# A four-layer graph network on one core: x by chunks of nodes, f1 through DRAM, and the last 20 keys in three copies

## Chip, core and metric

The kernel runs on one NeuronCore of a Trainium2 chip, in float32. The metric is the device time of one execution in microseconds. A profile is of one further execution; its engines are PE (TensorE's products, PEld its weight loads), DVE (VectorE), ACT (ScalarE), POOL (GpSimd) and SP (SyncE, which here only issues DMAs).

## The reference, cut to what matters

There are 2708 nodes with 512 features, a 0/1 adjacency matrix and four layers, each ended by a residual and a layer norm. Only layer 0 is changed. It has four heads of 128 features:

```python
Xw = einsum('hnd,hde->hne', Xh, W)            # 4 heads, 128 x 128 each
f1 = einsum('hnd,hd->hn', Xw, V[:, 0, :, 0])  # one number per node and head
f2 = einsum('hnd,hd->hn', Xw, V[:, 1, :, 0])
sig = sigmoid(f1[:, :, None] + f2[:, None, :])
att = masked_softmax(adj * sig, adj != 0)     # both patterns are adj
Xa = einsum('hij,hjd->hid', att, Xw)          # first attention pass
emb = mlp_block(batchnorm(Xa))                # x @ W.T, elu, residual, batch norm
Y = einsum('hij,hjd->hid', att, emb)          # second attention pass, same att
# times W.T per head, elu, a second mlp_block; then x = layernorm(x + out)
```

Layers 1 to 3 (a plain graph convolution, an attention masked by adj, an attention with adj as a bias) follow and are left as they are, but for one helper tile.

## The kernel before

The 2708 nodes make 22 blocks of 128 keys, the last of them with 20 (`BLOCKS`). Scores are held transposed: keys on the partitions, queries in the free dimension. The queries are cut in two halves of 1354 (`HSPAN`), a half in three chunks of 452, 450 and 452 (`HCH`, and `CHUNKS` for all six).

**project** (L186 to L251) makes what the attention needs. SP loads the small weights, then x transposed, as four transfers of one feature block with all 2708 nodes each (L197). From `w0T` and the two vectors it forms the products W·v (L200), and copies W·v1 to 128 columns (`wv1`, L205). Six float32 products with those columns (L210; a float32 product leaves two records in the trace, so twelve) give f1 of the first two heads and the first half directly broadcast over all 128 partitions, in `f1b`. For all six chunks, products with 32 of the columns (L218) give f1 in rows, and POOL's queue writes them to DRAM (`f1_d`, L227). Then, block by block, L232 gives xw with f2 beside it: ACT copies two of three blocks to `xw`, DVE the third (L240), and DVE keeps f2 in `f2h` (L244). Three PSUM buffers take turns.

**attention_pass** (L270) is run twice, with `xw` and then with `emb` as values. For each half `hf` and each pair of heads `p` it goes over the 22 key blocks. `form` (L294) loads the block's 0/1 rows `a` from adj transposed; in the first pass at p = 0 ("prepare") DVE turns zeros into -1e30 (L303, L304) and POOL's queue writes the result to `adj_d`, from which later rounds load. ACT forms tanh of f1 + f2 for both heads (L313), DVE adds and multiplies by `a` (L321), ACT takes the exponential (L322). The result `t` (four buffers) has 128 keys by 2 heads by 1354 queries. L366 multiplies it: two heads by three chunks, each accumulating in its own bank of PSUM over all 22 blocks. In the first pass, products with ones (L389) sum the exponentials: after each block at p = 0, after pairs of blocks else. A few `t` are kept in DRAM in the first pass and loaded back in the second (`KEPT`, L358 and L360; the last block is among them for every round of the second pass). `f1b` of every round but the first comes from `f1_d` by a broadcasting DMA (L330).

At the end of a round `keep` (first pass) copies the six banks to `ft` on DVE and ACT (L466), and `decode` (second pass) scales them on DVE (L660) and runs the following products and elus. The next round's products take the same six banks.

The last block's products in before, for any block:

```python
values[:n, jt, h * P : (h + 1) * P],
t[:n, k, q0 : q0 + qw],
```

With n = 20 they use rows 0 to 19 of the array. Layers 2 and 3 already hold the last 20 rows of their values in several copies, at partitions 0, 32, 64 and 96 (`values4`, L947 to L950), and multiply each copy in its own row group (L1090). A helper tile `quarters` is made from `ident` at L878 to L885.

The order on each engine comes from a scheduler over the tile framework; instructions of an engine run in that order, and each waits for semaphores. SP's DMAs are issued in SP's order. Tiles of one tag take turns in `bufs` buffers; `enc_w` (L183) shares its buffer with `held`, so its load waits for the last product that reads `held`.

Of the kernel before, what the change touches and what calls it, by code (L numbers as in the profile page):

```python
# [8 lines left out]
F32 = mybir.dt.float32  # L9
# [8 lines left out]
P = 128  # L18
# [11 lines left out]
def gnn_stack_kernel(  # L30
# [33 lines left out]

    const = ctx.enter_context(tc.tile_pool(name="const", bufs=1))
# [6 lines left out]
    nc.sync.dma_start(prm_sb, prm)  # L72
# [78 lines left out]
    with ExitStack() as l0:  # L151
# [20 lines left out]
        f2h = p0.tile([P, NT, H], F32, name="f2h")  # L172

        bm1 = p0.tile([P, C], F32, name="bm1")
        nc.vector.tensor_scalar(bm1, prm_sb[:, MB_DEC, :], 1.0, None, ALU.subtract)
        w0T_sb = p0.tile([P, H, P], F32, name="w0T_sb")
        nc.sync.dma_start(w0T_sb, w0T)
# [8 lines left out]
        def project(att, psum):  # L186

            held = p0.tile([P, C, F], F32, tag="mlp_w", name="held").rearrange("p c f -> p (c f)")  # L190
            w0x = held[:, : H * (P + 2)].rearrange("p (h e) -> p h e", h=H)
            nc.sync.dma_start(w0x[:, :, :P], w0)
            v12 = att.tile([P, H, 2], F32, tag="v12", name="v12", bufs=1)
            nc.sync.dma_start(v12[:, :, 0], v1)
            nc.sync.dma_start(v12[:, :, 1], v2.rearrange("(h e) -> e h", h=H))
            for c in range(C):
                nc.sync.dma_start(xT_sb[:, c, :], xT[c * P : (c + 1) * P, :])  # L197
# [6 lines left out]
            wv1 = held[:, H * (P + 2) : H * (2 * P + 2)].rearrange("p (h e) -> p h e", h=H)  # L204
            nc.vector.tensor_copy(wv1, w0x[:, :, P : P + 1].to_broadcast([P, H, P]))  # L205
            f1b = att.tile([P, HP, HW], F32, tag="f1b", name="f1b")
            for k in range(HP):
                for q, (q0, w) in enumerate(HCH[0]):
                    pf = psum.tile([P, HP, BANK], F32, tag=f"po{q}", name="pf")[:, k, :]
                    nc.tensor.matmul(  # L210
                        pf[:, :w], wv1[:, k, :], xT_sb[:, k, q0 : q0 + w], start=True, stop=True
                    )
                    copy = nc.scalar.copy if q % 2 else nc.vector.tensor_copy
                    copy(f1b[:, k, q0 : q0 + w], pf[:, :w])
            for ci, (c0, w) in enumerate(CHUNKS):
                pf = psum.tile([P, BANK], F32, tag=f"psm{ci % 2}", name="pf")
                for h in range(H):
                    nc.tensor.matmul(  # L218
                        pf[32 * h : 32 * h + 32, :w],
                        wv1[:, h, :32],  # L220
                        xT_sb[:, h, c0 : c0 + w],
                        start=True,
                        stop=True,
                    )
                f1c = att.tile([P, BW], F32, tag="rs", name="f1c")
                nc.vector.tensor_copy(f1c[:, :w], pf[:, :w])
                nc.gpsimd.dma_start(f1_d[:, c0 : c0 + w], f1c[0 : 32 * H : 32, :w])  # L227
# [23 lines left out]
            return f1b  # L251
# [18 lines left out]
        def attention_pass(values, first, att, psum, finish, f1b=None):  # L270
# [23 lines left out]
            def form(hf, p, jt, att, prepare, f1b, tv):  # L294
# [3 lines left out]
                a = att.tile([P, HW], F32, tag="a", name="a", bufs=4 if first else 3)  # L298
                src = adjT if prepare else adj_d
                nc.sync.dma_start(a[:n, :w], src[j0 : j0 + n, h0 : h0 + w])  # L300
                if prepare:
# [5 lines left out]
                    nc.gpsimd.dma_start(adj_d[j0 : j0 + n, h0 : h0 + w], a[:n, :w])  # L307
# [17 lines left out]
            for hf, (h0, w) in enumerate(HSPAN):  # L325
                for p in range(H // HP):
                    prepare = first and p == 0
                    if f1b is None or not prepare or hf > 0:
                        f1b = att.tile([P, HP, HW], F32, tag="f1b", name="f1b", bufs=2)
                        nc.sync.dma_start(  # L330
                            f1b[:, :, :w],
                            f1_d[HP * p : HP * (p + 1), h0 : h0 + w].partition_broadcast(P),
                        )
# [13 lines left out]
                    for jt, (j0, n) in enumerate(BLOCKS):  # L347
# [7 lines left out]
                        if kept is None or first:  # L355
                            form(hf, p, jt, att, prepare, f1b, tv)
                            if kept is not None:
                                nc.gpsimd.dma_start(kept[:n, :, :w], tv)  # L358
                        else:
                            nc.sync.dma_start(tv, kept[:n, :, :w])  # L360
                            if p == 0 and jt in KEPT[1]:
                                count(hf, jt, att)
                        for k in range(HP):
                            h = HP * p + k
                            for q, (q0, qw) in enumerate(HCH[hf]):
# [1049 lines left out]
```

## Time and profile before

| what | us |
|---|---|
| three runs | 3385.58, 3387.1, 3390.83 |
| their median | 3387.1 |
| the profiled execution, its own time | 3383.28 |
| its span, first to last instruction | 3381.5 |
| PE busy in the span | 3304.0 |
| first product of L366 starts at | 53.72 |
| L366 in the first pass, 1056 records, busy | 433.0 |
| L366 in the second pass, 1056 records, busy | 416.3 |
| DVE L321, 162 instructions, busy | 479.3 |
| mean granted PE clock (share of full speed) | 0.984 |

Times within the profile are counted from the span's start. Busy times of groups are unions, so overlapping records aren't counted twice, while the mean of one record is its own length; a PE record's end is modelled. A wait is put down to the engine or transfer whose signal came last.

### The profile page before, as it was taken

How to read it: one execution, taken by the hardware profiler on the slowest of the kernel's cores; microseconds unless marked ns; L12 is line 12 of the kernel's file. 1: busy time of each engine (PE TensorE's matmuls, PEld its weight loads, DVE VectorE, ACT ScalarE, POOL GpSimd, SP SyncE). 2: the span in 40 equal slices, each digit the busy share in tenths (PEclk: the TensorE clock that was granted, in tenths of full speed). 3: DMA queues.
4: the chain of work that ended last, by engine and by line, in shares of the span. 5: the costliest groups of instructions: out<-in, count | busy, mean ns of one | idle time of the engine just before them, and what ended most of it. 6: DMA issues, size and time to landing. Idle time of an engine off the chain costs nothing.

```text
span 3381.5 us, 30504 instructions
## 1 busy us (share of the span) xinstructions
PE 3304.0 (98%) x10981; PEld 1761.1 (52%) x10981; DVE 1988.8 (59%) x3227; ACT 1339.6 (40%) x1491; POOL 127.6 (4%) x205
## 2 busy tenths in 40 slices
PE   8999999999999989999999999999999999999998
PEld 4444444544444445886555555444455555555554
DVE  7867977767687585445136666777253442543533
ACT  6877887568858743001133333333011010110110
POOL 1100100000000000000010000000000000000001
PEclk9998999999999999999999999999999999999999
DMA  7655753335524331550034444554111111111100
GB/s 279 246 164 166 276 184 114 120 103 168 184 82 160 126 106 61 140 136 19 0 114 125 116 127 128 145 148 112 58 50 35 44 33 44 37 33 44 35 23 19
DMA packets 167483, 364.03 MB, mean 108 GB/s; under 512 B 20374, under 2 KB 111194, under 8 KB 164100
## 3 DMA queue, kind: packets, MB, share of 16 engines
q1 hardware_dynamic: 152596, 298.43, 29.3%
q0 software_dynamic: 14736, 63.66, 5.0%
q8 instruction: 86, 1.41, 0.2%
q14 instruction: 65, 0.53, 0.0%
HBM read 298.34 MB, written 63.35 MB: 107 GB/s over the span
## 4 chain that ended last, share of the span: by engine, by line
PE 74%; issue 15%; DVE 6%; DMA 2%; ACT 2%; POOL 1%; SPq 0%; POOLq 0%; DVEq 0%; ACTq 0%
PE po L1090 22%; PE ps_s L996 17%; PE po L366 8%; PE ps_nb L842 7%; PE ps_wide L908 4%; PE ps_hid L113 2%; PE ps_sup L1233 2%; DVE t L321 2%; PE ps_o L1168 2%; PE ps_dec L687 2%; PE ps_mlp L601 1%; DMA a<-adj_d 1%; POOL adj_d L307 1%; PE ps_s L991 1%; ACT t L313 1%
## 5 line engine op out<-in xcount | busy, mean ns | idle before, releaser
L321 DVE SCALAR_TENSOR_TENSOR t<-t,a 128x2708 f32<-128x2708 f32 (+1 forms) x162 | 479.3, 2975 | 144.8 <-ACT t L313 143.3
L313 ACT ACTIVATE t<-f1b,f2h 128x1354 f32<-128x1354 f32 (+1 forms) x324 | 445.3, 1414 | 91.2 <-PE psm L389 47.1
L366 PE MATMUL po<-t,xw 128*128 128x452 f32 (+3 forms) x1056 | 433.0, 561 | 3.9 <-ACT t L322 3.9
L366 PE MATMUL po<-t,emb 128*128 128x452 f32 (+3 forms) x1056 | 416.3, 552 | 10.7 <-ACT t L322 9.2
L322 ACT ACTIVATE t<-t 128x2708 f32<-128x2708 f32 (+1 forms) x162 | 396.7, 2452 | 52.0 <-DVE t L321 50.5
L1090 PE MATMUL po<-sup,e 128*128 128x512 f32 x882 | 410.0, 601 | 5.2 <-DVE e L1277 5.2
L1090 PE MATMUL po<-e,xs 128*128 128x384 f32 (+1 forms) x1176 | 407.5, 489 | 0.0
L996 PE MATMUL ps_s<-q,hT 128*128 128x384 f32 (+1 forms) x1176 | 403.5, 489 | 0.0
L1331 DVE SCALAR_TENSOR_TENSOR e<-a_cols,ps_s 128x384 f32<-128x384 f32 (+1 forms) x154 | 85.6, 556 | 419.7 <-PE ps_s L996 396.6
L366 PEld LDWEIGHTS po<-t,emb 128*128 128x128 f32 (+1 forms) x1056 | 201.6, 193 | 220.1 <-issue 199.2
L366 PEld LDWEIGHTS po<-t,xw 128*128 128x128 f32 (+1 forms) x1056 | 197.8, 193 | 224.9 <-issue 211.4
L996 PEld LDWEIGHTS ps_s<-q,hT 128*128 128x128 f32 x1176 | 222.6, 190 | 161.5 <-issue 6.2
L1090 PEld LDWEIGHTS po<-e,xs 128*128 128x128 f32 x1176 | 221.6, 190 | 157.2 <-issue 6.0
L1090 PEld LDWEIGHTS po<-sup,e 128*128 128x128 f32 x882 | 162.0, 192 | 176.8 <-issue 148.3
L996 PE MATMUL ps_s<-hT 128*128 128x384 f32 (+1 forms) x672 | 229.2, 488 | 1.0 <-ACT sup L1240 0.7
L93 ACT ACTIVATE ln_rstd<-ln_rstd 128x1 f32<-128x1 f32 x88 | 17.2, 201 | 497.4 <-DVE ln_rstd L92 496.9
L1273 ACT ACTIVATE a_cols<-a_cols,neg_big 128x384 f32<-128x384 f32 (+1 forms) x154 | 94.8, 616 | 249.7 <-DMA a_cols<-in_adjT_dram 208.4
L842 PE MATMUL ps_nb<-hid_hi,at 128*128 128x512 f32 x484 | 188.1, 390 | 0.4 <-DVE at L836 0.4
L842 PE MATMUL ps_nb<-hid_lo,at 128*128 128x512 f32 x484 | 187.8, 389 | 0.0
L1067 ACT COPY nmax<-pb 128x384 f32<-128x384 f32 (+1 forms) x14 | 6.7, 479 | 430.5 <-PE pb L1054 349.8
L996 PEld LDWEIGHTS ps_s<-hT 128*128 128x128 f32 x672 | 125.8, 190 | 97.1 <-issue 18.0
L1085 DVE TENSOR_TENSOR acc<-acc,e 128x384 f32<-128x384 f32 (+2 forms) x294 | 162.9, 554 | 12.3 <-ACT e L1075 2.3
(223 smaller groups left out, 3474.1 us busy)
## 6 DMA issues: line engine op xcount, KB each, us to landing
a<-adj_d SPq DMA_DIRECT2D x116, 677.0 KB
a_cols<-in_adjT_dram SPq DMA_DIRECT2D x378, 192.0 KB
a<-in_adjT_dram SPq DMA_DIRECT2D x42, 677.0 KB
adj_d<-a POOLq DMA_DIRECT2D x42, 677.0 KB, 4.5
raw<-in_adjT_dram SPq DMA_DIRECT2D x105, 256.0 KB
kept<-t POOLq DMA_DIRECT2D x10, 1354.0 KB, 6.6
t<-kept SPq DMA_DIRECT2D x10, 1354.0 KB
a_cols<-in_adjT_dram SPq DMA_DIRECT2D x63, 202.0 KB
```

The lines of the kernel that those rows point to most:

```text
L113: nc.tensor.matmul(ps[:n], xt[:, c, :n], w[:, c, :], start=(c == 0), stop=(c == C - 1))
L313: nc.scalar.activation(tv[:, k, :], f1b[:n, k, :w], AF.Tanh, bias=f2h[:n, jt, h : h + 1], scale=0.5,)
L321: nc.vector.scalar_tensor_tensor(tv, tv, GUARD, ab, ALU.add, ALU.mult)
L322: nc.scalar.activation(tv, tv, AF.Exp, scale=0.5)
L366: nc.tensor.matmul(po[HB * k + q][:, :qw], values[:n, jt, h * P : (h + 1) * P], t[:n, k, q0 : q0 + qw], start=(jt == 0), stop=(jt == NT - 1),)
L842: nc.tensor.matmul(pos[it], at, half[:, jt, :], start=(jt == 0 and k == 0), stop=(jt == NT - 1 and k == 1),)
L908: nc.tensor.matmul(ps[:, :width], w(c, o), xt(c), start=(c == 0), stop=(c == C - 1),)
L996: nc.tensor.matmul(ps[:, :w], keys[:, c, j0 : j0 + P], st["q"][:, c, :], start=(c == 0), stop=(c == C - 1),)
L1085: nc.vector.tensor_tensor(acc, acc, e[:m], ALU.add)
L1090: nc.tensor.matmul(out, lhsT, rhs, start=(k == 0), stop=(k == NT - 1))
L1273: nc.scalar.activation(a, a, AF.Identity, bias=neg_big[: a.shape[0]], scale=1.0e30)
L1331: nc.vector.scalar_tensor_tensor(e, a, 2.0, ps, ALU.mult, ALU.add)
```

## The change

Three things are done in layer 0.

- **x and the vectors.** The two vectors are the first loads, then the weights, then x in six chunks of nodes with all features of each (one transfer a chunk), with the first two blocks of `a` put between them. `prm` comes after that.
- **f1.** The broadcast products of L210 are gone. f1 of the first three chunks is formed in rows first, then all blocks of xw, then f1 of the other three. The first three chunks go to DRAM by SP's queue, the others by POOL's, and `f1b` of every round, the first too, comes back by a broadcasting DMA.
- **The last 20 keys.** xw, f2h and emb of the last block get two more copies at partitions 32 and 64, made by DMAs on POOL's queue from one part of SBUF to another. The tile `a` of the last block is loaded in three copies, with rows of other keys to fill the 12 rows between them; tanh, the vector steps and the exponential then run on 84 rows. A kept `t` is loaded three times. Of the products of a head, chunk q uses copy q, in rows 32q to 32q + 19.

The tile `quarters` moves from the pool that lives throughout to one that opens after layer 1.

The diff, cut to its core (`Q` = 32, `REST` = 20, `HB` = 3, `HR` = 84):

```diff
+        nc.vector.memset(f2h[:, NT - 1, :], 0.0)
+        HR = (HB - 1) * Q + REST
+        def copies(rows):
+            for r in range(1, HB):
+                nc.gpsimd.dma_start(rows[r * Q : r * Q + REST], rows[:REST])
...
-            nc.sync.dma_start(w0x[:, :, :P], w0)
             v12 = att.tile([P, H, 2], F32, tag="v12", name="v12", bufs=1)
-            nc.sync.dma_start(v12[:, :, 0], v1)
             nc.sync.dma_start(v12[:, :, 1], v2.rearrange("(h e) -> e h", h=H))
-            for c in range(C):
-                nc.sync.dma_start(xT_sb[:, c, :], xT[c * P : (c + 1) * P, :])
+            nc.sync.dma_start(v12[:, :, 0], v1)
+            nc.sync.dma_start(w0T_sb, w0T)
+            nc.sync.dma_start(w0x[:, :, :P], w0)
+            blocks = []
+            for ci, (c0, w) in enumerate(CHUNKS):
+                nc.sync.dma_start(
+                    xT_sb[:, :, c0 : c0 + w],
+                    xT[:, c0 : c0 + w].rearrange("(c p) j -> p c j", p=P),
+                )
+                if HB - 1 <= ci and len(blocks) < 2:
+                    j0 = P * len(blocks)
+                    a = att.tile([P, HW], F32, tag="a", name="a", bufs=4)
+                    nc.sync.dma_start(a[:, : HSPAN[0][1]], adjT[j0 : j0 + P, : HSPAN[0][1]])
+                    blocks.append(a)
+            nc.sync.dma_start(prm_sb, prm)
+            nc.vector.tensor_scalar(bm1, prm_sb[:, MB_DEC, :], 1.0, None, ALU.subtract)
...
-            f1b = att.tile([P, HP, HW], F32, tag="f1b", name="f1b")
-            for k in range(HP):
-                for q, (q0, w) in enumerate(HCH[0]):
-                    pf = psum.tile([P, HP, BANK], F32, tag=f"po{q}", name="pf")[:, k, :]
-                    nc.tensor.matmul(
-                        pf[:, :w], wv1[:, k, :], xT_sb[:, k, q0 : q0 + w], start=True, stop=True
-                    )
-                    copy = nc.scalar.copy if q % 2 else nc.vector.tensor_copy
-                    copy(f1b[:, k, q0 : q0 + w], pf[:, :w])
-            for ci, (c0, w) in enumerate(CHUNKS):
+            def f1_rows(ci):
...
-                nc.gpsimd.dma_start(f1_d[:, c0 : c0 + w], f1c[0 : 32 * H : 32, :w])
+                queue = nc.sync if ci < HB else nc.gpsimd
+                queue.dma_start(f1_d[:, c0 : c0 + w], f1c[0 : 32 * H : 32, :w])
+            for ci in range(HB):
+                f1_rows(ci)
             for jt, (j0, n) in enumerate(BLOCKS):
...
-            return f1b
+            for ci in range(HB, NCH):
+                f1_rows(ci)
+            copies(xw[:, NT - 1, :])
+            copies(f2h[:, NT - 1, :])
+            return blocks
...
+                if n < P:
+                    for r in range(HB):
+                        if r > 0:
+                            nc.sync.dma_start(
+                                a[r * Q : r * Q + n, :w], src[j0 : j0 + n, h0 : h0 + w]
+                            )
+                        if r + 1 < HB:
+                            nc.sync.dma_start(
+                                a[r * Q + n : (r + 1) * Q, :w], src[: Q - n, h0 : h0 + w]
+                            )
+                    n = HR
...
-                    if f1b is None or not prepare or hf > 0:
-                        f1b = att.tile([P, HP, HW], F32, tag="f1b", name="f1b", bufs=2)
+                    f1b = att.tile([P, HP, HW], F32, tag="f1b", name="f1b", bufs=2)
...
-                            nc.sync.dma_start(tv, kept[:n, :, :w])
+                            for r in range(0, P if n == P else HB * Q, P if n == P else Q):
+                                nc.sync.dma_start(t[r : r + n, :, :w], kept[:n, :, :w])
...
+                                r = 0 if n == P else q * Q
                                 nc.tensor.matmul(
                                     po[HB * k + q][:, :qw],
-                                    values[:n, jt, h * P : (h + 1) * P],
-                                    t[:n, k, q0 : q0 + qw],
+                                    values[r : r + n, jt, h * P : (h + 1) * P],
+                                    t[r : r + n, k, q0 : q0 + qw],
...
+            copies(emb[:, NT - 1, :])
...
-    quarters = const.tile([P, C, Q], F32, name="quarters")
+    quarters = featp.tile([P, C, Q], F32, name="quarters")
```

## The prediction

> I call one run over the 22 key blocks for one half of the columns and one pair of heads a quarter: A1 to A4 are those of the first attention pass in the kernel's order, B1 to B4 those of the second. Line numbers are those of the kernel before.
>
> **What bounds the kernel now.** First the page's busy times:
>
> ```profile
> PE 3304.0 (98%) x10981; PEld 1761.1 (52%) x10981; DVE 1988.8 (59%) x3227; ACT 1339.6 (40%) x1491; POOL 127.6 (4%) x205
> ```
>
> TensorE nearly always has work, so time goes only where PE work goes, runs faster, or waits less. The change touches layer 0, up to about 1240 us. So second, the waits there: from 53 to 620 us PE waits 6.3 us in all, and ScalarE waits for PE:
>
> ```profile
> PE po L366 <- ACT t L322: 3.9, 6, 1.2
> ...
> ACT t L313 <- PE psm L389: 47.1, 42, 6.2
> ```
>
> (total, times, longest.) Pass A is PE's. From 680 to 1240 us PE waits 9.2 us for the exponentials (L322) and 7.9 us for the decoder's vector chain: in pass B, PE and ScalarE are close.
>
> Third, PE's timeline at the end of A1 (start, duration, ..., shape, records; a float32 product leaves two records), and the windows around it, where the third number from the right is the granted clock:
>
> ```profile
> 176.07 1.35 PE L389 MATMUL psm<-t,ones 128*32 128x340 f32 x16
> 177.35 5.89 PE L366 MATMUL po<-t,xw 20*128 20x452 f32 x12
> 183.17 2.49 PE L389 MATMUL psm<-t,ones 20*32 20x340 f32 x16
> ```
> ```profile
> 177.00:180.00 3.00, 3.00 (x15) 1.40 (x8) 0.21 (x1) 2.76 (x2) 0.00 (x0) 1.00 0.58 175
> 181.00:185.00 4.00, 4.00 (x20) 1.03 (x18) 2.41 (x5) 2.18 (x4) 0.00 (x0) 0.50 0.01 1
> 185.00:190.00 5.00, 5.00 (x14) 2.19 (x7) 4.38 (x4) 3.58 (x3) 1.17 (x2) 0.50 0.04 4
> 191.00:196.00 5.00, 5.00 (x27) 2.14 (x26) 1.28 (x2) 2.11 (x3) 0.00 (x0) 0.98 0.77 259
> ```
>
> The 20-key block takes no less than a full one (12 records at 0.38 us are 4.6), and after it PE, busy throughout, is granted half its clock for ten microseconds. Windows of 1 us over all eight quarters show the same each time: half clock at 181 to 191, 311 to 328, 454 to 464, 584 to 588, 812 to 816, 922 to 925, 1075 to 1079 and 1181 to 1188 us, always as such a block ends.
>
> Fourth, the same 20 keys in layer 2, where three copies already lie in different row groups:
>
> ```profile
> 1829.26 1.45 PE L996 MATMUL ps_s<-hT 128*128 128x384 f32 x4
> 1830.65 1.13 PE L1090 MATMUL po<-values,e 20*128 20x512 f32 x6
> 1831.71 1.24 PE L996 MATMUL ps_s<-hT 128*128 128x384 f32 x3
> ```
>
> Six records in 1.06 us (to the next start); a full 512-wide record costs 410.0/882 = 0.465 us in the groups, so six in turn would be 2.8. No half-clock stretch begins at any such block of layers 2 and 3.
>
> Fifth, the start: first product of L366 at 53.72, the x loads filling 6 to 19.5 us, and the broadcast f1:
>
> ```profile
> 11.11 6.24 PE L210 MATMUL pf<-xT_sb,held 128*128 128x452 f32 x8 [2.26 <-DVE quarters L883]
> 28.67 2.75 ACT L313 ACTIVATE t<-f1b,f2h 128x1354 f32<-128x1354 f32 x2
> ```
>
> **What the Trainium skill says.** "TensorE: Matmul & The Clock Gate", part 3 (packing small matmuls): products in different row groups run at once; four of K=32 gave 3.07 times. The trace agrees: 2.8/1.06 = 2.6 for three. The same page, part 1 (the HAM clock gate): an activity window of about 3.4 us that counts as idle halves the clock, a busy one restores it. The stretches here (3.4 to 17 us) fit the window; but PE was not idle, so the trace widens it: 4.6 us of 20-row products pass for idle. "DMA: Bandwidth & Descriptors", latency and other measured facts: about 2 us fixed cost for a DMA; the list of DMA issues has 2.3 us from issue to landing for the f1 rows to DRAM.
>
> **The change part by part.**
>
> *1. Packed last block.* For each pair of heads, three products in row groups 0, 32, 64. Scaled from 1.06 us at 512 columns to 452: 0.95, two heads 1.9 us. Time from its first record to the next PE instruction before: A 5.8, 5.4, 6.4, 4.9; B 4.8, 5.5, 5.5, 7.9 (the last three with waits). Removed at full clock: 4.9 - 1.9 = 3.0 a quarter, 24 in all.
>
> *2. The half clock.* The weak stretch shrinks from 4.6 to 1.9 us, plus 1.35 of 20-row sums in A1 and A3: 3.25, under a window. I take it that the clock stays. What it costs now, A: the excess of the block over 4.9 (0.9, 0.5, 1.5, 0), of the 16 sums (2.49 against 1.35, each time 1.1), of the next products (twelve in 7.6 for 4.8 us in A1; 2.0 in A3; in A2 3.3 and the 32 one-column products of L434, 6.8 for 3.5), A4 0.4: 4.8, 8.2, 4.6, 1.5, sum 19. B: half of the 3.4, 3.4, 3.4 us and some of the last: 6. The value could be zero if 20 rows in each of three groups still count as idle.
>
> *3. What takes it back.* Evacuation of po begins when the block ends; before, it ran under the slow block. At A1's end ScalarE has 11.8 us of tanh and exponentials queued ahead of its L466 copies (171.4 to 183.2), so the next quarter's second bank is late by about 1.4 us; A2 and A3 alike. A2 is short of t near its end (waits of 0.47 us before L366), which eats 2 to 3 us of a faster start. Of 12 + 19 = 31 in pass A I keep 24. In pass B DVE needs 3.7 us for the six L660 evacuations: it can give back about 2.1, 1.5, 1.5 and 0.6 of the 3.0 each; with the clock's 6 this is 12, and ScalarE being near its limit I keep 7.
>
> *4. Work for the copies.* tanh, STT and exp on 84 rows instead of 20 take the same time (a 20-row tanh pair 2.74, a 128-row one 2.74). The a tile comes by five SP transfers instead of one; a kept t tile by three. Buffers are asked for some three blocks (16 us) ahead, which hides four more issues of 0.3 to 0.4 us and the filling; bare they'd cost 1.5 us each. POOL's SBUF copies of xw and f2h stand ahead of its adj_d write of block 2 and of two f1 writes, priced in 5. emb's copies have a quarter to land.
>
> *5. The start.* Removed: 12 records of L210, 8.8 us at the low clock. Vectors first: v lands at 5.3 instead of 7 (issued 1.6 us earlier). x chunks at about 390 GB/s (the x chunks of layer 1 in the trace) land at 8.0, 10.3, 12.7, then a block of a, and the last at 23. PE: f1 rows from 8, blocks of xw at 1.0 us (24 records in 2.95), 2.0 while the clock is low till about 13; so xw ends at 36 instead of 53.7. But in the changed program's order ScalarE does all xw copies before its first tanh, and DVE copies the third f1 chunk only after 17 of the 22 f2 steps, about 32. Then f1 to DRAM (2.3), issue, broadcast of 1354 KB behind a block of a (5.4 us from issue before): about 41.5. On DVE the first STT stands behind the last f1 copy, whose buffer waits for POOL's f1 write, itself behind POOL's copy of the last xw rows: about 42. Then two tanh 2.8, STT 3.0; the first exp behind five tanh: 48.5 + 2.5 = 51. Before, PE came to 53.7 with two blocks of sums done (2.7 us) and warm; now it idles from 38.6 to 51 and starts cold (a half to one window lost, 2.6). 51 + 2.7 + 2.6 - 53.7: 3 us later. Between -4 (f1 copied early) and +6.
>
> *6. quarters* leaves the start and lies in layer 2's first normalisations: 12 small steps of 0.1 us, partly in gaps: +0.5.
>
> Sum: -24 - 7 + 3 + 0.5 = -27.5. The profiled execution took 3383.3 (span 3381.5 and 1.8 around it) and would become 3356; it lies 3.8 under the median of the runs shown, from which I forecast 3387.1 - 28 = 3359.
>
> **The rivals.** *All of it counts:* 24 + 25 with nothing given back, a start without loss: 3338. For it: PE 98% busy; against: L660 and L466 stand right behind. *Clock stays low or the ends absorb it:* only 12 to 15 us of packing remain and the start costs 3: 3376. For it: in pass B PE already waits. *The packing does nothing:* if the products don't overlap, the start is all: 3390; against it layer 2. *Slower:* SP issues the five transfers of a last block one landing after another, 2.1 us each: 8.4 us more, and next quarter's a tiles queue behind. With less than 4 us of lead this stops PE in A1 to A4, and four more landings for the kept t hit B1 to B4: 4 x 8.4 + 4 x 4.2 = 50 against 28: 3409. Against it: SP has up to three blocks of lead.
>
> **How the numbers follow.** This measurement tells about 0.2% (6.8 us) from no change. Main case 0.58 (3347 to 3370), all counts 0.15, absorbed 0.18, packing does nothing 0.05, slower 0.04. The first three are faster, the fourth the same (its upper end and a small gain included), so 0.91, 0.05, 0.04. The range 3340 to 3376 leaves out most of the last two and the tails.
>
> **What would show it.** Right: 12 records of 20 rows in about 1.9 us at each quarter's end, no 0.50 clock there, first product of L366 near 51 with PE idle before it, L434's products in 3.5 us. Wrong: half-clock stretches still at the ends (step 2); PE idle over 3 us at each quarter's start (step 3); first product past 57 or before 46 (step 5); SP waits before a at the ends (slower).

## The result and the profile after

| kernel | median us | runs | ratio to before, 95% interval |
|---|---|---|---|
| before | 3387.07 | 20, 3378.80 to 3396.04 | 1 |
| after | 3392.43 | 20, 3385.48 to 3404.19 | 1.0017 [1.0008, 1.0027] |

The forecast was 28 us less; it became 5 us more, which the interval just tells from no change. The median of the kernel before moved between 3382 and 3387 us from one set of runs to another, so the ratios below, each to the kernel before in the same set, are what is compared. The profiled execution took 3388.89 us (span 3386.8, mean clock 0.983). Its busy times, first line of the page:

```profile
PE 3264.8 (96%) x10969; PEld 1744.0 (51%) x10969; DVE 1984.8 (59%) x3224; ACT 1339.4 (40%) x1489; POOL 130.0 (4%) x208
```

TensorE works 39 us less than before and the span is 5 us longer: PE's idle time has grown by 44 us, 13 of them ahead of its first product of L366. The packing and the loss of L210 did take work away; waits filled the room. The end of A1 in after, PE's timeline (start, duration, records; in brackets the wait ahead and what ended it):

```profile
179.76 1.79 PE L408 MATMUL po<-t,xw 20*128 20x452 f32 x12
181.47 1.35 PE L431 MATMUL psm<-t,ones 20*32 20x340 f32 x16
184.02 1.36 PE L408 MATMUL po<-t,xw 128*128 128x452 f32 x2 [1.20 <-DVE ft L508]
188.83 6.98 PE L408 MATMUL po<-t,xw 128*128 128x452 f32 x10 [3.45 <-ACT ft L508]
```

and windows over the same stretch (length, busy time of PE, PEld, DVE, ACT and POOL, granted clock, DMA share, GB/s):

```profile
178.00:181.00 3.00, 3.00 (x27) 1.11 (x28) 3.00 (x2) 2.58 (x3) 0.00 (x0) 1.00 0.19 51
181.00:184.00 3.00, 1.82 (x22) 0.41 (x17) 3.00 (x4) 2.57 (x2) 0.00 (x0) 1.00 0.76 240
184.00:188.00 4.00, 1.36 (x2) 0.29 (x2) 1.82 (x5) 4.00 (x4) 1.16 (x2) 0.56 0.45 160
188.00:195.00 7.00, 6.17 (x9) 2.97 (x10) 6.18 (x3) 5.76 (x5) 0.00 (x0) 0.52 0.34 103
```

The block takes 1.71 us (179.76 to 181.47), not 5.8. Then PE waits 1.20 us for the bank that VectorE empties, two records later 3.45 for ScalarE's, and is at half clock again for ten microseconds. From this block's start to the second block of A2 (197.02) it is 17.3 us, before it was 17.0. In pass A PE's waits are now led by the copies of L508 (L466 before):

```profile
PE po L408 <- ACT ft L508: 6.5, 2, 3.4
...
PE po L408 <- ACT t L362: 4.1, 7, 1.0
```

Pass B, PE's waits from 690 to 1240 us (L362, L715, L448 and L703 are L322, L672, L406 and L660 before):

```profile
PE po L408 <- ACT t L362: 16.2, 11, 4.4
PE ps_y L719 <- DVE ot L715: 7.5, 3, 4.3
PE ps_y L719 <- DVE elu_r L448: 6.1, 5, 3.4
PE po L408 <- DVE ot L703: 4.8, 2, 3.3
PE ps_dec L730 <- DVE elu_r L448: 1.8, 3, 1.3
```

These are 36.4 us, 17.1 by the same five lines before (9.2, 3.7, 1.6, 1.4, 1.2). And the start:

```profile
37.57 0.96 PE L233 MATMUL pf<-xT_sb,held 128*32 128x450 f32 x8
51.57 6.41 PE L408 MATMUL po<-t,xw 128*128 128x452 f32 x12 [13.04 <-ACT t L362]
```

The first product of L366 starts at 51.57 (forecast 51), after 13 us of idle, at half clock, as forecast. In the traces of the other four kernels with this start (front_only, quarters_early, after_keep1, pad_front, all below) it starts between 51.62 and 54.11.

By stage, from PE's timelines, each column against the kernel before (us; the last three are kernels of the next section):

| stage | forecast | after | pack_only | pack_keep1 | pad_rows |
|---|---|---|---|---|---|
| to A1's last block | +3 | +2.4 | -1.6 | -2.0 | -1.3 |
| to the MLP's first product (L578) | -24 | -10.9 | -10.8 | -10.0 | -17.5 |
| MLP, to B1's first product | 0 | +4.1 | 0.0 | +4.0 | 0.0 |
| pass B, to the last decoder product | -7 | +8.0 | +6.7 | -3.1 | -7.3 |
| the rest | +0.5 | +1.7 | +0.1 | -3.9 | +0.5 |
| sum (span) | -27.5 | +5.3 | -5.7 | -15.0 | -25.6 |

pack_only, pack_keep1 and pad_rows share the start of the kernel before, so the 1.3 to 2.0 us by which they lead at A1's last block show how far one trace can be trusted there. Inside the quarters the steps from block to block are mostly the same in all kernels (6.03 us in A1 and A3, 4.55 to 4.66 in pass B); what differs lies where one quarter passes into the next.

### The profile page after: what moved, and what is told of

It is laid out like the page before. It is cut to its first block, busy times and chain, and to the rows that moved or that the text cites. A ratio compares the mean times of both kernels' runs of the same rounds, so it can differ in the third digit from the quotient of the medians.

```text
span 3386.8 us, 30539 instructions
## 1 busy us (share of the span) xinstructions
PE 3264.8 (96%) x10969; PEld 1744.0 (51%) x10969; DVE 1984.8 (59%) x3224; ACT 1339.4 (40%) x1489; POOL 130.0 (4%) x208
## 3 DMA queue, kind: packets, MB, share of 16 engines
q8 instruction: 86, 1.41, 0.2%
## 4 chain that ended last, share of the span: by engine, by line
PE 72%; issue 15%; DVE 6%; DMA 2%; ACT 2%; POOL 1%; SPq 0%; POOLq 0%; DVEq 0%; ACTq 0%
PE po L1128 22%; PE ps_s L1034 17%; PE ps_nb L885 6%; PE po L408 6%; PE ps_wide L946 4%; DVE t L361 3%; PE ps_hid L117 2%; PE ps_sup L1271 2%; PE ps_o L1206 2%; PE ps_mlp L643 2%; DMA a<-adj_d 1%; PE ps_dec L730 1%; ACT t L362 1%; ACT t L353 1%; POOL adj_d L347 1%
## 5 line engine op out<-in xcount | busy, mean ns | idle before, releaser
L361 DVE SCALAR_TENSOR_TENSOR t<-t,a 128x2708 f32<-128x2708 f32 (+1 forms) x162 | 478.7, 2974 | 147.8 <-ACT t L353 146.1
L408 PE MATMUL po<-t,xw 128*128 128x452 f32 (+3 forms) x1056 | 419.1, 560 | 24.8 <-ACT t L362 17.1
L362 ACT ACTIVATE t<-t 128x2708 f32<-128x2708 f32 (+1 forms) x162 | 396.6, 2452 | 67.4 <-DVE t L361 67.0
L408 PE MATMUL po<-t,emb 128*128 128x452 f32 (+3 forms) x1056 | 402.0, 551 | 21.0 <-ACT t L362 16.2
```

The source lines that it names most:

```text
L361: nc.vector.scalar_tensor_tensor(tv, tv, GUARD, ab, ALU.add, ALU.mult)
L362: nc.scalar.activation(tv, tv, AF.Exp, scale=0.5)
L408: nc.tensor.matmul(po[HB * k + q][:, :qw], values[r : r + n, jt, h * P : (h + 1) * P], t[r : r + n, k, q0 : q0 + qw], start=(jt == 0), sto ...
```

## The experiments

My theory after this: packing shortens the block as forecast, but the block stands where banks are emptied, so its gain comes back as waits; and short block plus waits still pass for idle, so the half clock stays. Rivals: the new start costs it all; the half clock has nothing to do with the 20 rows; the order of instructions changed.

### Which part costs: pack_only, front_only, quarters_early

pack_only is the kernel before with the last block in three copies alone; front_only the changed kernel without it; quarters_early the changed kernel with `quarters` in its old pool.

```diff
 # front_only: every packed line back to
-                                r = 0 if n == P else q * Q
+                                r = 0
 # quarters_early and front_only
-    quarters = featp.tile([P, C, Q], F32, name="quarters")
+    quarters = const.tile([P, C, Q], F32, name="quarters")
```

> The kernel before with the three copies of the last 20 keys alone; x, f1 and quarters as before. Theory E (the ends of the quarters are set by the evacuation of the six banks and by the order on ACT and DVE, so the 3 us that PE saves come back as PE idle): the 20-row products take 1.7 us, PE then idles 1 to 5 us at the start of each next quarter, and the time stays within 8 us of the kernel before, pass B a little longer (+3 to +8 us). Rival F (the start and quarters cost what packing gained): 12 us or more faster, near 3375.

> The changed kernel without the three copies and with quarters where it was: chunks of x, vectors first, f1 through DRAM. Both theories: the first product of the attention near 51 to 52 us, the last block of A1 2 to 3 us later than before. Theory E: +2 to +3 us in all. Rival F, where the start is the whole loss: +5 us or more.

> The changed kernel with quarters back in the pool that lives throughout. The trace of the changed kernel loses 2.0 us between the last neighbour product of layer 1 and the end of layer 2's projections. If quarters among the last normalisations is the cause: 2 us faster than the changed kernel, that is 3 us over the kernel before. If not: no difference.

Measured: pack_only 3381.9 us, 0.9994 [0.9983, 1.0005]; front_only 3389.85, 1.0014 [1.0006, 1.0021]; quarters_early 3389.74, 1.0017 [1.0009, 1.0025]. Packing alone is worth nothing that shows (theory E: PE waits 1.2 to 3.1 us around the ends of pass A, and pass B is 6.7 us longer), the start alone costs some 5 us (2 to 7 by the interval, so it doesn't decide between the two theories of that run), and the place of `quarters` nothing (the ratio is that of after). So the missing gain is not hidden by the start: it is missing in the packing itself.

### What halves the clock: pad_rows, pad64, mid20, mid_pack

pad_rows undoes packing and start, and fills the last block to 128 rows (zeros in xw and emb, so the result is the same): as long as a full block, all rows at work. pad64 fills it to 64 rows.

```diff
+                if n < P:
+                    nc.gpsimd.memset(xw[:, jt, :], 0.0)
...
-                                    values[:n, jt, h * P : (h + 1) * P],
-                                    t[:n, k, q0 : q0 + qw],
+                                    values[:, jt, h * P : (h + 1) * P],
+                                    t[:, k, q0 : q0 + qw],
```

> The kernel before with the last block filled up to 128 rows: its values have zeros in rows 20 to 127 and its exponentials are those of other keys, so the products are full ones of 4.6 us with the same sums. It asks what the half clock costs. Theory C (the 20-row products are what halves the clock, since they count as idle): no half clock at the ends of A1 to A4 and B1 to B3, and 10 to 20 us faster than before, near 3372. Theory E: the clock may stay up, but only what the evacuation lets through is gained, 5 us or more still, because the slow block no longer hides less than before. If the clock falls here too, the rows are not the cause: within 3 us of before.

> As pad_rows, but the last block is padded with zero rows to 64 rows only; the added terms are zero. Theory A (the clock gate counts how much of the array works, and 64 rows are enough to count as busy): no half clock at the ends, 3357 to 3361 as pad_rows. Rival (the gate wants more than half of the rows, or counts by share so that 64 rows pass for idle like 20): half-clock stretches at the eight ends as in the kernel before, 3380 to 3386.

Measured: pad_rows 3359.01 us, 0.9930 [0.9916, 0.9944]; pad64 3363.07, 0.9941 [0.9929, 0.9954]. The end of A1 in pad_rows, PE's timeline:

```profile
176.08 4.82 PE L373 MATMUL po<-t,xw 128*128 128x452 f32 x12
180.83 1.35 PE L396 MATMUL psm<-t,ones 20*32 20x340 f32 x16
182.11 4.82 PE L373 MATMUL po<-t,xw 128*128 128x452 f32 x12
```

No wait, no slow record: the same twelve records with more rows, and 24 us of the whole time gone, more than the 10 to 20 expected. In windows of 1 us seven of the eight ends have no half clock; at A2's end one stretch of 3.4 us is left, with 32 one-column products (L434) before it. With 64 rows four of eight ends still have a stretch (3.4 to 6.8 us), so neither theory of pad64 came as stated. But none of the four stands behind 64-row products alone: at A1's and A3's end 20-row sums (L389) follow at once, at A2's the one-column products, at B4's a wait of 2.84 us. Where 64-row products fill a window of 3.4 us by themselves, as at B2's end, the clock stays:

```profile
903.37 4.81 PE L373 MATMUL po<-t,emb 64*128 64x452 f32 x12
```
```profile
903.91:907.32 3.41, 3.41 (x11) 1.67 (x10) 3.27 (x2) 3.09 (x3) 0.00 (x0) 1.00 0.00 0
```

What remained open was whether packed rows count as idle by themselves. In mid20 the 20-key block changes places with the twelfth one, in the order of keys and among the kept t; mid_pack packs it there.

```diff
-    KEPT = [(5, 13, 21), (3, 9, 15, 21)]
+    KEPT = [(5, 13, 11), (3, 9, 15, 11)]
+    ORDER = list(range(NT))
+    ORDER[11], ORDER[NT - 1] = NT - 1, 11
...
-                    for jt, (j0, n) in enumerate(BLOCKS):
+                    for i, jt in enumerate(ORDER):
+                        j0, n = BLOCKS[jt]
```

> The kernel before with the 20-key block and the twelfth block exchanged in the order of the keys: the 20-key block stands in the middle of each quarter, not packed and not padded, between full blocks with nothing to evacuate; the twelfth block takes its place at the end, and among the kept t. Theory A (20-row products by themselves count as idle): each of the eight quarters has a half-clock stretch of 3.4 to 7 us after the twelfth place, none but that of the one-column products at its end; the time comes 5 to 15 us under the kernel before, 3370 to 3382, since fewer products stand in the slow stretch. Rival (the end of a quarter does it, by evacuation and short waits): no half clock in the middle, stretches at the ends as in the kernel before; the time within 5 us of it.

> The same exchange with the 20-key block packed in three row groups (a kept t comes by one DMA). Theory A (packed rows are well enough when full products stand before and behind; the gain of pack_keep1 was lost because the short block stood ahead of the banks' evacuation, where a wait of TensorE completes an idle window): no half clock in the middle or at the ends, the 3 us a quarter stay in the first pass, and the time is 3336 to 3350, under pad_rows' 3359. Rival 1 (the packed block still passes for idle): a stretch of 3.4 us in most middles, 3355 to 3365. Rival 2 (the forming of t is the limit, so that 3 us saved in the middle of a quarter come back as waits for the exponentials): no half clock, but waits of 2 to 3 us more a quarter, 3354 to 3360.

Measured: mid20 3379.66 us, 0.9989 [0.9979, 0.9999]; mid_pack 3360.1, 0.9940 [0.9926, 0.9953]. The middle of A1 in mid20, PE's timeline and then windows:

```profile
116.03 4.81 PE L367 MATMUL po<-t,xw 20*128 20x452 f32 x12
120.77 2.18 PE L390 MATMUL psm<-t,ones 20*32 20x340 f32 x16
122.88 7.33 PE L367 MATMUL po<-t,xw 128*128 128x452 f32 x12
```
```profile
116.00:121.00 5.00, 5.00 (x20) 2.29 (x20) 3.34 (x4) 4.83 (x3) 0.77 (x1) 1.00 0.51 171
121.00:128.00 7.00, 7.00 (x23) 2.88 (x16) 6.79 (x4) 5.25 (x4) 1.28 (x3) 0.51 0.91 331
178.00:188.00 10.00, 10.00 (x52) 4.28 (x51) 6.17 (x8) 8.98 (x8) 1.14 (x2) 1.00 0.31 106
```

The stretch has moved with the block: half clock in the middle of seven quarters (in B1 and B3 3.4 us of it was there before, now 6.8 and 10), none at the end but that of the one-column products. The 20 rows do it, without any wait. The time fell by 3 us, less than the 5 to 15 expected. Packed (mid_pack), it depends on the wait behind. A1 and A3, PE's timeline, then windows over both:

```profile
116.51 1.79 PE L394 MATMUL po<-t,xw 20*128 20x452 f32 x12
118.22 1.35 PE L417 MATMUL psm<-t,ones 20*32 20x340 f32 x16
119.50 4.82 PE L394 MATMUL po<-t,xw 128*128 128x452 f32 x12
...
376.64 1.79 PE L394 MATMUL po<-t,xw 20*128 20x452 f32 x12
378.36 1.35 PE L417 MATMUL psm<-t,ones 20*32 20x340 f32 x16
381.98 7.72 PE L394 MATMUL po<-t,xw 128*128 128x452 f32 x12 [2.28 <-ACT t L348]
```
```profile
116.00:120.00 4.00, 4.00 (x39) 1.42 (x31) 3.93 (x4) 3.36 (x2) 0.72 (x1) 1.00 0.63 214
120.00:125.00 5.00, 5.00 (x24) 2.30 (x26) 4.52 (x4) 4.58 (x5) 1.25 (x2) 1.00 0.91 367
...
381.00:387.00 6.00, 5.02 (x7) 2.52 (x8) 5.83 (x4) 5.91 (x4) 0.53 (x1) 0.50 0.80 236
```

In this trace the packed block keeps the clock with no wait behind it (A1) and with waits of 1.27 and 1.26 us (B2, B4), and loses it with 1.8 to 2.3 us of waits ahead of it and behind (A2, A3, A4; B1 and B3 too). The kernel before has stretches of 3.4 us behind waits of 2.15 and 2.03 us between full blocks (B1 at 754, B3 at 1020). But the length of the wait alone doesn't decide. mid_pack_chunks (last part of this section) has the same packed block in A4 and the same wait, 2.00 us for 2.01, and keeps the clock. The windows over both, mid_pack first:

```profile
507.31:510.72 3.41, 1.81 (x13) 0.70 (x12) 3.41 (x2) 2.97 (x2) 0.00 (x0) 1.00 0.44 122
510.72:514.13 3.41, 3.00 (x17) 1.10 (x18) 3.41 (x3) 2.87 (x3) 0.00 (x0) 0.50 0.20 81
```
```profile
501.29:504.70 3.41, 3.17 (x16) 1.07 (x14) 3.41 (x2) 3.00 (x3) 0.00 (x0) 1.00 0.13 17
504.70:508.11 3.41, 1.65 (x17) 0.71 (x18) 3.41 (x2) 2.93 (x3) 0.00 (x0) 1.00 0.49 186
```

In every trace here the changes of clock lie whole multiples of 3.413 us apart. In mid_pack block and wait fall into one such stretch, in mid_pack_chunks an edge parts them. Between 45 and 1200 us the 17 traces have 5494 such stretches at full clock, and 149 of them are followed by half clock. An estimate from these stretches: a record counts with the share of the 128 rows it uses (20 rows 0.16, 64 rows 0.5, three packed copies 60/128 = 0.47), a one-column product and idle time with nothing. A bound of 1.41 us per stretch then separates all but ten; those ten count 1.23 to 1.61. Half clock follows below the bound (mid_pack above: 1.79 us of packed products, 0.84), not above it (the two of mid_pack_chunks: 2.22 and 1.66; B2's of pad64: 1.71). With packed rows counted as full rows 30 are wrong, as idle 36, with only idle time counted 99, each at the bound that suits it best.

So packed rows pass neither for idle nor for full work: a packed block alone keeps the clock, and the waits around it take it when they fall into the same stretch. That the hardware counts in this way isn't shown, only that this count fits.

The waits in mid_pack are for the exponentials and for the sum of two t: 20.5 and 3.2 us in the two passes, where mid20 has 11.6 and none, so part of the 24 us saved on PE comes back because t isn't formed faster. Theory A failed: five of eight middles have half clock, as rival 1 had it, and the 3336 to 3350 didn't come. 3360 lies within rival 1's range and at the edge of rival 2's, whose waits came too.

### What takes the packing's gain back: pack_dve, pack_keep1, after_keep1

pack_dve is pack_only with all six copies of L466 on VectorE. pack_keep1 is pack_only with the last block's t kept in all its 84 rows and loaded by one DMA instead of three (so the store is larger too); after_keep1 is the changed kernel with that.

```diff
 # pack_dve
-                        copy = nc.scalar.copy if q % 2 else nc.vector.tensor_copy
+                        copy = nc.vector.tensor_copy
 # pack_keep1, after_keep1
-                                nc.gpsimd.dma_start(kept[:n, :, :w], tv)
+                                nc.gpsimd.dma_start(kept[:rows, :, :w], t[:rows, :, :w])
...
-                            for r in range(0, P if n == P else HB * Q, P if n == P else Q):
-                                nc.sync.dma_start(t[r : r + n, :, :w], kept[:n, :, :w])
+                            rows = n if n == P else HR
+                            nc.sync.dma_start(t[:rows, :, :w], kept[:rows, :, :w])
```

> pack_only with all six end-of-quarter bank copies of pass A (L466) put on VectorE, so that none stands behind ScalarE's tanh and exponentials. Theory A (the ScalarE copies are what the packed block runs into, and the wait on them also fills an idle window): the 3.1 to 3.5 us waits for ACT ft vanish, the ends of A1 and A3 show at most one half-clock window each, and the time falls by 4 to 9 us under pack_only's 3381.9, to 3373 to 3378. Rival 1 (the six copies in a row on VectorE take as long as the wait they replace, about 3.6 us for six): the wait moves to DVE ft and the time stays at 3380 to 3384. Rival 2 (pass B decides, where A's gain is lost anyway): A ends 5 us or more earlier, the total stays at 3380 to 3384.

> pack_only, but the last block's t is kept in DRAM with all its 84 rows and comes back by one DMA, not three. With that, the instructions of VectorE and ScalarE in the second pass stand in the order of the kernel before (second vector step of the next quarter's t ahead of the six L660 and of the elu chain); with three DMAs the scheduler put them behind. Theory A (the changed order is what takes packing's gain and more in the second pass: pack_only lost 6.7 us there where the sum had -7): the second pass gains 2 to 7 us against the kernel before, and the time falls 8 to 14 us under pack_only, to 3368 to 3374. Rival (the waits for the evacuation on VectorE and for ot come whatever the order, and the clock falls with them): within 3 us of pack_only, 3379 to 3384.

> The changed kernel with the same single DMA for a kept t of the last block, and nothing else changed. Theory A (order in the second pass): 8 to 14 us under the changed kernel, 3378 to 3384, which brings it just under the kernel before; what then stays against the prediction is the half clock and the start. Rival (order does nothing): 3388 to 3393 as the changed kernel.

Measured: pack_dve 3381.5 us, 0.9998 [0.9990, 1.0006]. At A1's end the wait is 0.52 us and the clock stays; at A3's end VectorE has a 2.98 us step for the next t ahead of the copies, PE waits 5.12 us for them, and the clock halves; at A2's end it waits 3.95 us for them. Pass A gains no more than in pack_only: rival 1. pack_keep1: 3368.56, 0.9959 [0.9945, 0.9973]; after_keep1: 3383.73, 0.9997 [0.9988, 1.0006]. One DMA in place of three took some 12 us off pack_only, as expected, and 7 off the changed kernel, where 8 to 14 were expected. No wait of PE is for a kept t's DMA in any of these; what differs is the order. VectorE from B3 to B4 in after:

```profile
1071.16 1.28 DVE L703 SCALAR_TENSOR_TENSOR ot<-po,bn_scale,rb 128x452 f32<-128x452 f32 x2 [5.96 <-PE po L408]
1072.36 0.68 DVE L715 SCALAR_TENSOR_TENSOR ot<-ot,bn_shift,linked 128x452 f32<-128x452 f32 x1
1072.96 2.46 DVE L703 SCALAR_TENSOR_TENSOR ot<-po,bn_scale,rb 128x452 f32<-128x452 f32 x4
...
1081.88 0.62 DVE L448 TENSOR_SCALAR elu_r<-ps_y 128x452 f32<-128x452 f32 x1
1082.42 2.97 DVE L361 SCALAR_TENSOR_TENSOR t<-t,a 128x2708 f32<-128x2708 f32 x1
```

and in pack_keep1, where the order is that of the kernel before:

```profile
1060.74 2.98 DVE L345 SCALAR_TENSOR_TENSOR t<-t,a 128x2708 f32<-128x2708 f32 x1 [4.35 <-ACT t L337]
1063.64 3.66 DVE L688 SCALAR_TENSOR_TENSOR ot<-po,bn_scale,rb 128x452 f32<-128x452 f32 x6
1067.21 3.08 DVE L700 SCALAR_TENSOR_TENSOR ot<-ot,bn_shift,linked 128x452 f32<-128x452 f32 x5
```

With three loads of the kept t the scheduler places the next quarter's step on t (L361) behind nearly the whole elu chain; VectorE stands idle 5.96 us ahead of the evacuation, and B4's next exponential (L362) starts at 1085.4 where before it had run at 1072.7. PE then waits 4.35 us for it and the clock halves. So the second pass lost 6.7 us in pack_only, and gains 3.1 in pack_keep1.

### The start: pad_front, pad_chunks, chunks_alone

With clean ends a start can be measured. pad_front is the changed start and place of `quarters` on the padded block; pad_chunks is pad_rows with the changed loads (vectors first, x in chunks of nodes, prm last), but f1 of the first half broadcast by TensorE (L210, chunk by chunk); chunks_alone is the kernel before with those loads.

```diff
 # pad_chunks, chunks_alone
-            for c in range(C):
-                nc.sync.dma_start(xT_sb[:, c, :], xT[c * P : (c + 1) * P, :])
+            for c0, w in CHUNKS:
+                nc.sync.dma_start(
+                    xT_sb[:, :, c0 : c0 + w],
+                    xT[:, c0 : c0 + w].rearrange("(c p) j -> p c j", p=P),
+                )
...
-            for k in range(HP):
-                for q, (q0, w) in enumerate(HCH[0]):
+            for q, (q0, w) in enumerate(HCH[0]):
+                for k in range(HP):
```

> The changed start (vectors first, x in chunks of nodes, f1 of the first half through DRAM) and the changed place of quarters, with the last block padded to 128 rows of zeros as in pad_rows and without the packing. The padding adds terms of zero only. Theory A (the new start itself costs a few microseconds, whatever the ends do: front_only stood +2.7 us in A1 and about +5 us by the median against the kernel before): 3362 to 3366, that is 3 to 7 us over pad_rows' 3359. Rival (what front_only lost came from where half-clock stretches fell afterwards, and the start is neutral): 3358 to 3360, same as pad_rows.

> pad_rows with the loads of the changed start (vectors first, x in chunks of nodes, prm last), but f1 of the first half still broadcast by TensorE, chunk by chunk, as in the kernel before. Theory A (what costs in the new start is the way of f1 through DRAM, with ScalarE's copies ahead of the first tanh; earlier x alone helps): TensorE starts about 3 us earlier and the time is 3355 to 3358, 1 to 4 us under pad_rows. Rival (the start is bound by the copies of xw on ScalarE and VectorE and the first exponentials, not by the loads): 3358 to 3361, same as pad_rows.

> The kernel before with the loads of the changed start alone (vectors first, x in chunks of nodes, prm last); f1 of the first half is still broadcast by TensorE, and the last block is as before. Theory A (the loads help and the way of f1 through DRAM is what costs, as pad_chunks and pad_front showed on clean ends): 3 to 7 us under the kernel before, 3375 to 3382. Rival (the gain of pad_chunks came from where clock windows fell): same as the kernel before within 2 us.

Measured: pad_front 3367.13 us, 0.9956 [0.9943, 0.9969]; pad_chunks 3353.37, 0.9913 [0.9900, 0.9925]; chunks_alone 3381.94, 0.9994 [0.9985, 1.0004]. Against pad_rows (0.9930) the changed start costs 9 us, more than I expected of it, and the loads alone bring 6 by the ratios, more than the 1 to 4 expected, though these two intervals overlap. On the kernel before they show nothing that the interval can tell from none, though its A1 is 3.4 us ahead: the half-clock stretches in that trace are longer (windows of 1 us from 40 to 1260 us: 106 us of half clock, 75 before; that execution, 3387.97, was among the slowest of its thirteen). Of the 9 us, 6.3 are there at A1's last block (182.40 against 176.08), though A1's first product is just 1.7 us later (54.11 against 52.45): the sums of the first two blocks, 2.7 us, now stand behind it, and it runs at half clock until 57.6. More is lost at the end of A1, on ScalarE in pad_front:

```profile
183.01 2.46 ACT L353 ACTIVATE t<-t 128x2708 f32<-128x2708 f32 x1 [0.41 <-DVE t L352]
185.90 2.46 ACT L353 ACTIVATE t<-t 128x2708 f32<-128x2708 f32 x1 [0.43 <-DVE t L352]
188.27 2.72 ACT L344 ACTIVATE t<-f1b,f2h 128x1354 f32<-128x1354 f32 x2
190.90 0.95 ACT L499 COPY ft<-po 128x452 f32<-128x452 f32 x2
```

The copies start 8.5 us after the last block (182.40); in pad_rows they start 4.9 after it (180.97, block at 176.08). PE waits 2.45 us for them and falls to half clock. ScalarE and VectorE are late because t has no lead. From the end of a block's exponential to its first product, pad_rows has 14.1 us at the first block and 6.3 to 8.1 in mid-quarter; with the new start, where PE takes up each t as it comes, it is 0.1 at the first block and 0.8 to 5.1 over the last eight. The lead isn't won back within the quarter, though VectorE works only 25.1 of 30 us from 90 to 120 us there. From 60 to 182 us ScalarE waits 20.9 us for VectorE's step on t (5.3 in pad_rows), and VectorE waits 11.6 us for loads of `a` (4.6 in pad_rows); SP, before these loads, waits for the step on an earlier t (L352), the last reader of a buffer of `a`. So each step on t holds up the load for a later one. Whether more buffers of `a` would give the lead back wasn't tried.

### The best of each: pack_keep1_chunks, mid_pack_chunks

pack_keep1 and mid_pack, each with the loads of chunks_alone.

```diff
+                    xT_sb[:, :, c0 : c0 + w],
+                    xT[:, c0 : c0 + w].rearrange("(c p) j -> p c j", p=P),
```

> pack_only with one DMA for a kept t of the last block, and with the loads of the changed start (vectors first, x in chunks of nodes): all that helped so far around the packed block, f1 by TensorE. If the packed block were worth more than the padded one once order and start are right, this beats pad_chunks' 3353. Theory A (packing saves 3 us a quarter, but with the end's waits still loses clock windows that padding keeps): 3363 to 3371, better than the kernel before, 10 to 18 us behind pad_chunks. Rival (order was all): 3345 to 3353.

> mid_pack with the loads of the changed start (vectors first, x in chunks of nodes), f1 by TensorE. Theory A: 3 to 6 us under mid_pack, 3330 to 3346, the best so far and under pad_chunks' 3353. Rival (the start's gain is lost in the first quarter, as in chunks_alone): same as mid_pack within 2 us.

Measured: 3363.07 us, 0.9946 [0.9931, 0.9962], and 3358.07, 0.9930 [0.9918, 0.9943]. The first is at the edge of theory A's range. mid_pack_chunks is 2 us under mid_pack by the medians and misses its range; neither reaches pad_chunks (its interval and that of mid_pack_chunks overlap), which at 0.9913 is the fastest kernel of this study, 29 us under the kernel before, with a block of 128 rows that are mostly zeros.

## Why the prediction was wrong, step by step

*Step 1, the packed block: right.* 12 records in 1.71 us for 1.9 forecast, 3 us less than a full block; PE's busy time fell.

*Step 2, the half clock: the assumption failed, the price held.* "I take it that the clock stays", since 1.9 us of packed products and 1.35 of sums are "under a window". The sum left out the waits behind the block, which fall into the same stretch of 3.4 us as the thin rows: at A1's end in after 1.20 us of idle, 1.72 of packed products and 20-row sums and 0.5 of full rows. Half clock at the eight ends went from 58 us to 44 (windows of 1 us). The 25 us that I priced the half clock at were there to be had: pad_rows, which aims at nothing else, gained 24 [19, 28].

*Step 3, what takes it back: the mechanism right, the size wrong.* The bank that ScalarE empties was to be late by about 1.4 us in A1, A2 and A3; PE waited 3.45 us for it at A1's end in after (1.76 in pack_only) and 3.07 at A3's end in both, and such a wait costs clock as well. The 11.8 us read as queued ahead of the copies (171.4 to 183.2) include the 0.95 us of the copies themselves. Of 31 us in pass A I kept 24; 10.8 came in pack_only, 10.9 in after.

*Step 4, the copies: failed where it looked safest.* "a kept t tile by three" was costed as transfers hidden by a lead of three blocks, and the transfers are hidden. But three DMAs changed the scheduler's order on VectorE and ScalarE in the second pass; pack_keep1 prices that at 12 us (0.9959 against 0.9994). Where 7 us less was forecast, pass B took 8.0 more in after; of the 9.8 us between pack_only and pack_keep1 there, none is a wait of PE for these transfers. The prediction used the order of the changed program for the start only.

*Step 5, the start: the first product right in the changed kernel's trace (51.57 for 51; 51.6 to 54.1 in all five), the cost too small.* A1's last block came 2.4 us later (4.0 against pack_only, forecast 3; 6.3 in pad_front). The rest falls due at A1's end, a term that the sum didn't have: a lead of 14 us had gone. The products of L210 that fell away took 8.0 us, not 8.8, and the last four of them ran at full clock; the sum of this step didn't use the figure. On clean ends it is 9 us (pad_front against pad_rows), and 13 between after_keep1 and pack_keep1, which includes the place of `quarters`.

*Step 6, quarters:* 0.5 forecast, nothing to be measured.

The rival that came nearest was the one in which the ends absorb the gain and the clock stays low (3376, 0.18); order and start then took more than the 12 to 15 us that it left to the packing. The slower rival's mechanism was not seen: PE waits for no DMA of `a` at the ends.

In after the one-column products of the MLP (L434 and the next) lost 4.1 us to half clock, for which the forecast had nothing. It came with pack_keep1 and chunks_alone too, which don't have the new start, and not with pad_front, which has it. It follows from where the edges of the 3.413 us stretches fall: one with 2.19 us or more of one-column products is followed by half clock (2.19 at 611 us in after), one with 2.18 or less isn't (2.18 at 603 us in pack_keep1_chunks, 2.15 at 618 us in before). Where they fall there was neither forecast nor chosen in any of these kernels, so that these 4 us are chance.

*Open.* How a kernel could place its thin blocks against these edges, and whether more buffers of `a` mend the start.

## What to carry to other kernels

A block with few rows is cheap only if the clock stands it: look at the granted clock behind every thin block, add up thin rows and waits that stand close together, and try full rows of zeros before packing, since they add no wait. Shortening the last block before a change of buffers hands its time to whoever empties the buffers; price their queue first. Compare the order of instructions in every stage that an edit's DMAs or tiles touch, not only where the edit aims, and when work is moved to an earlier start, ask what lead the next engine had.

## What was not expected of the hardware

- TensorE without a gap in its records falls to half clock when the products use 20 rows: eight of eight ends before, seven of eight middles in mid20. The eighth (A4) has 2.42 and 2.33 us of thin rows on the two sides of an edge; by the count above these are 1.38 and 1.45, at the bound. With 128 rows one end of eight falls, behind one-column products. The Trainium skill, "TensorE: Matmul & The Clock Gate", part 1, speaks of windows of about 3.4 us and of idle ones; the stretches here are indeed multiples of 3.413 us on a fixed grid, but here few rows at work count as mostly idle too, by their share of 128, as far as 5494 stretches tell; the page doesn't say so, and the measurements decide.
- Idle time well under a window is enough: between full blocks 1.97 us and more within one stretch cost the clock, 1.94 and 1.96 did not (pack_only at 810, after at 1017 us); in the decoder 1.80 and 1.81 us did, twice.
- The half clock goes with the spread: over the 20 runs of after the mean granted clock lies between 0.980 and 0.985 and the time correlates with it at -0.87; 0.001 of mean clock is 6.8 us at half clock, or 3.4 us of time. Where the stretches at half clock fall differs from run to run.
